# Ten tiles turned by VectorE in 32 by 32 blocks instead of by TensorE

## The chip, the core and the metric

The kernel runs on one core of one Trainium2 chip. The metric is the device time of one execution in microseconds (us). Engines are named as in the profile: PE is TensorE (PEld its weight loads), DVE is VectorE, ACT is ScalarE, POOL is GpSimd, SP is the engine that only issues transfers. PSUM is the memory that PE writes to, SBUF the working memory.

## What is computed

A graph attention layer on 2708 nodes of width 1024, all in fp32:

```
h   = relu(layernorm(x))
z   = (h Wq' + bq) (h Wk' + bk)' / 32            # only where adj is not 0
out = x + relu(softmax(z * adj, else -10000) (h Wv' + bv))
```

adj is 0 or 1 with about 4 ones in a row, so the kernel never forms the 2708 by 2708 matrix.

## The kernel before, in words

**Algebra.** Wq and Wk are first multiplied into one matrix M, so that q = h M is all that the scores need. For each node the rows h of its neighbours are gathered, their scores are dot products with q, and u is the weighted sum of those same rows. The result is u Wv. So two matrix products of 2688 by 1024 by 1024 remain on PE: "q units" (h M) and "o units" (u Wv).

**Tiles and units.** Nodes are sorted by degree and cut into 21 full tiles of 128 rows and a short one. Units 0 to 9 are q units, units 10 to 19 are o units, each with a pair of tiles. The o pairs follow the list `order` (L928): (6,5), (4,3), (2,0), (1,7) are units 10 to 13, (13,12), (11,10), (14,9), (15,16) units 14 to 17, (20,17) and (18,19) units 18 and 19. Tile 8 is `alone` and comes last.

**One unit.** A unit is a Strassen product of a 2 by 2 block of tiles: seven products of 8 PE instructions each. `multiply` (L982) runs them in this order, and calls `after(0)` to `after(6)` (L1172) around them: s2 (into bank Y), a12 (X), s4 (Z), s3 (Y), then a11 and s1 of the next unit (`opened`, L953), then a22 (Y). The left operands are made in the unit before by `blocks` (L677). Its `upper`, called at `after(0)`, turns tile xa: PE transposes eight 128 by 128 blocks into PSUM (`half_turned`, L397), and ACT copies them out as a11 and a12. Its `lower`, called at `after(2)`, does the same for xb; ACT copies a22 alone, and DVE makes s1 = a22 + a21 and s3 = a11 - a21 with a21 read from PSUM, then s2 = s1 - a11 and s4 = a12 - s2. In q units 1 and 2, s2 and s4 are made by POOL (`eng`, L701 and L702); in all later units by DVE.

**The results of a unit.** c11 and c21 leave their bank by ACT; c12 (L1063) is a DVE addition that reads bank Z, c22 (L1059) a DVE addition behind an ACT copy. There are four banks for X, Y, Z. The copy that starts bank Y of the next unit (`opened`, L961, on ACT) takes the bank that c12 sets free.

**The stream on DVE.** Scores (L826), weights (L840 to L873) and sums (L879) of all tiles form one sequence of steps, `attention` (L897), which `advance` (L937) deals out between the products: `share`, that is 19/7 us of estimated step time, at each `after` of an o unit. Each score is a pass over 1024 columns with two operands in SBUF (a gathered row block g and q), each sum another (g and u). The order of DVE's instructions is the order in which this code writes them (L1165); the other engines' order in units 4 to 19 is chosen by the scheduler. The first term of u is written by ACT (L871). POOL issues the gathers (L597) into 13 buffers; a gather waits for the step that read its buffer last.

**Keeping or reloading u.** When the last sum of tile t is done, `near` (L933) asks whether the tile's unit is at most two units ahead. If so, u stays in SBUF (`held`). If not, SP stores it to `u_dram` (L888) and `load_rows` (L1130) brings it back with one transfer of 128 rows of 4 KB (L1142). Ten tiles go that way: 6, 5, 4, 3, 2, 0, 1 and 20, 18, 19. `load_rows` for unit n+2 is called at `after(4)` of unit n, and before it a loop (L1214) advances the stream until both tiles are done, whatever `share` says. Rows live in seven buffers of 4 KB (`row_tile`, L198).

Of the kernel before, what the change touches and what calls it, by code (L numbers as in the profile page):

```python
# [15 lines left out]
ALU = mybir.AluOpType  # L16
AX = mybir.AxisListType

P = 128
# [13 lines left out]
NONE = 1e-30  # L33
FAR = 20.0
WIDE = 8
MOMENTS = (0, 1, 2, 3, 6, 7)
ROOT = 32
WARM = 11
# [25 lines left out]
def tile_preln_masked_attention(  # L64
# [12 lines left out]
    nc = tc.nc  # L77
    N, D = x.shape
# [25 lines left out]
    u_dram = dram.tile([FULL * P, D], FT, name="u_dram")  # L104
# [61 lines left out]
    t = 0  # L166
    while t < NT:
# [4 lines left out]
        t = e  # L172
# [25 lines left out]
    def row_tile(name):  # L198
        return work.tile([P, D], FT, tag="row", name=name, bufs=ROWS)
# [197 lines left out]
    def half_turned(xt, s):  # L397

        pt = psum.tile([P, 4, P], FT, tag="tp", name="pt")
        for c in range(4):  # L400
            k = s * 4 + c
            nc.tensor.transpose(pt[:, c, :], xt[:, k * P:(k + 1) * P], ident)  # L402
        return pt
# [187 lines left out]
    def small(name):  # L591
        return half.tile([P, NB], FT, tag="half", name=name, bufs=14)
# [8 lines left out]
    rows_of = {}  # L601
    FIRST = EARLY // 2
# [71 lines left out]

    behind = []

    def blocks(xa, xb, eng=None):  # L677


        ops = {}  # L680

        def held(name, bank):
            ops[name] = small(name).rearrange("p (c q) -> p c q", q=P)
            nc.scalar.copy(ops[name], bank)  # L684

        def put(name, a, b, op, eng=None):
            ops[name] = small(name).rearrange("p (c q) -> p c q", q=P)
            step = (eng or nc.vector).tensor_tensor(ops[name], a, b, op=op)  # L688
            if eng is None:
                behind.append(step)  # L690

        def upper():
            held("a11", half_turned(xa, 0))
            held("a12", half_turned(xa, 1))

        def lower():
            held("a22", half_turned(xb, 1))
            a21 = half_turned(xb, 0)
            put("s1", ops["a22"], a21, ALU.add)
            put("s3", ops["a11"], a21, ALU.subtract)  # L700
            put("s2", ops["s1"], ops["a11"], ALU.subtract, eng)  # L701
            put("s4", ops["a12"], ops["s2"], ALU.subtract, eng)  # L702

        return ops, upper, lower
# [170 lines left out]
    def sums(t):  # L875
        u, coef = us.pop(t)
        for s in range(0 if t in EMPTY else 1, K[t]):
            fill()
            chained(lambda: nc.vector.scalar_tensor_tensor(  # L879
                u, g_of[t][s], coef[:, at[t][s]:at[t][s] + 1], u, op0=ALU.mult, op1=ALU.add))  # L880
            free.append(g_of[t][s])
            yield 1.3
        fill()
        g_of.pop(t)
        if near(t):
            held[t] = u
        else:
            nc.sync.dma_start(u_dram[t * P:(t + 1) * P, :], u)  # L888
        done.add(t)
# [43 lines left out]
    def near(t):  # L933

        return t == alone or any(t in unit[1:] for unit in units[:now[0] + 3] if unit[0] == "o")
# [194 lines left out]
    def load_rows(unit):  # L1130
        kind, *pair = unit
        rows = []
        for t in pair:
            if t in held:
                rows.append(held.pop(t))
                continue
            rows.append(row_tile(f"{kind}r_{t}"))
            if kind == "q":
                gather(rows[-1], h_dram[:, :], t, SLOTS, P)
            else:  # L1140
                assert t in done, (t, done)
                nc.sync.dma_start(rows[-1], u_dram[t * P:(t + 1) * P, :])  # L1142
        return rows

    products = []
# [14 lines left out]
    for n, unit in enumerate(units):  # L1160
        kind, ta, tb = unit
        now[0] = n
        if n == FIRST:
            ordered.close()
            ordered.enter_context(tc.manual_schedule(engines={mybir.EngineType.DVE}))  # L1165
            nc.sync.dma_start(bp_dram, bp_sb[0:1, :])
        turn = n in (0, FIRST - 1)
        share = (20.0 if kind == "q" else 19.0) / 7
        nxt = units[n + 1] if n + 1 < len(units) else None
        results = (q_results if kind == "q" else o_results)(ta, tb)  # L1170

        def after(i):  # L1172
            if (n, i) in steps_ahead:
                follow(steps_ahead[n, i])
            if (n, i) == (2, 5):
                owe(8)
                owe(9)
                rows_of[FIRST] = load_rows(units[FIRST])
                owe(10)
                owe(6)  # L1180
                owe(7)
                rows_of[FIRST + 1] = load_rows(units[FIRST + 1])
                pooled.close()
            if (n, i) in ((FIRST, 1), (FIRST, 5)):
                ts_of_wv(i // 2, i // 2 + 2)
            if (n, i) == (FIRST, 5):
                next(stream)
            if (n, i) == (FIRST, 6):
                chain.append(behind[-1])
                next(stream)  # L1190
                nc.vector.tensor_tensor(bad, bad, total, op=ALU.not_equal)
            if (n, i) == (FIRST + 1, 6):
                marked(EARLY, NT)
            if (n, i) == (FIRST + 2, 4):
                nc.vector.tensor_scalar(msq, msq, MLIMIT, None, op0=ALU.is_gt)
            if n > FIRST + 1 or n == FIRST + 1 and i > 1:
                advance(share)
            if nxt is not None:

                if i == (3 if n == 0 else 4 if turn else 0):  # L1200
                    ops_of[n + 1] = blocks(*rows_of[n + 1], nc.gpsimd if n + 1 < FIRST - 1 else None)
                    with tc.issue_after(products[-1].ins) if n + 1 == FIRST else nullcontext():
                        ops_of[n + 1][1]()
                if i == (4 if n == 0 else 5 if turn else 2):
                    ops_of[n + 1][2]()
                    rows_of.pop(n + 1)
                    if n == last_q - 1:
                        all_rows()
                if i == 3:
                    banks_of[n + 1] = banks_for(bp_sb)  # L1210
                if i == 6 and n + 2 < FIRST:
                    natural_rows(n + 2)
                if i == (2 if n in (FIRST, last_q) else 4) and n + 2 > FIRST and n + 2 < len(units) and n + 2 not in rows_of:
                    while units[n + 2][0] == "o" and not done.issuperset(units[n + 2][1:]):  # L1214
                        advance(1.0)
                    rows_of[n + 2] = load_rows(units[n + 2])
            if (n, i) in steps_at:
                follow(steps_at[n, i])
            if (n, i) == (3, 4):
                searched()  # L1220
            if (n, i) == (3, 5):
                for s in range(8, HIGH):
                    for c in range(0, D, D // 4):
                        clear = nc.gpsimd.memset(slots[s][:, c:c + D // 4], 0.0)
                        tc.add_manual_dep(clear.ins, counted_at[-1].ins.name,
                                          mybir.DependencyInfo(mybir.DependencyClass.Sync, mybir.DependencyReason.DATA),
                                          reason="not beside the counts")
            if i == 3 and units[n - 1][0] == "o" and NT - 2 in units[n - 1][1:]:
                tail(NT - 1)
            if nxt is None and i == 1:  # L1230
                while alone not in done:
                    advance(1.0)
                r, = load_rows(("o", alone))
                single["turned"] = turned(r, "alone")
            if nxt is None and i == 3:
                single["banks"] = banks_for(bp_sb)
            if n == last_q - 1 and i == 4:

                nc.sync.dma_start(bp_sb, bv.to_broadcast([P, D]))
                nc.vector.tensor_sub(bp_sb[:, NB:], bp_sb[:, NB:], bp_sb[:, :NB])  # L1240

            for k, at in enumerate(((0, 0), (0, 1), (0, 3), (0, 4), (0, 5), (0, 6), (1, 2))):
                if (n - last_q, i) == at:
                    place, src = ((M[:, 0, 0], of_wv(0, 0)), (T[:, 0], tv_dram[0]), (T[:, 1], tv_dram[1]),
                                  (M[:, 1, 0], of_wv(1, 0)), (M[:, 1, 1], of_wv(1, 1)), (T[:, 2], tv_dram[2]),
                                  (T[:, 3], tv_dram[3]))[k]
                    nc.sync.dma_start(place, src)

        multiply(n, results, after)
# [231 lines left out]
```

## Time and profile before

| | |
|---|---|
| median of 3 runs | 644.58 us (644.18 to 644.96) |
| profiled execution, first to last instruction | span 641.9 us; no total is listed for this execution |
| busy: PE, DVE, POOL, ACT | 635.2, 521.9, 377.3, 279.6 us of the span |
| PE's granted clock | 9 of 10 or more in all 40 slices (mean 0.998) |
| DMA engines | 315 GB/s over the span |

An o or q unit lasts 25.78 us on PE: unit 9 begins at 346.70 us of the span, unit 19 at 604.55 us. In the rows of the profile, a line begins with its time and duration or with its source line and engine; `out<-in` are the program's tile names, xN is a count, and what stands in brackets or behind "<-" is how long the engine had been idle and what released it. `pt<-ident,or` are the transposes of reloaded tiles, `pt<-ident,u` those of held ones.

### The profile page before, as it was taken

How to read it: one execution, taken by the hardware profiler on the slowest of the kernel's cores; microseconds unless marked ns; L12 is line 12 of the kernel's file. 1: busy time of each engine (PE TensorE's matmuls, PEld its weight loads, DVE VectorE, ACT ScalarE, POOL GpSimd, SP SyncE). 2: the span in 40 equal slices, each digit the busy share in tenths (PEclk: the TensorE clock that was granted, in tenths of full speed). 3: DMA queues.
4: the chain of work that ended last, by engine and by line, in shares of the span. 5: the costliest groups of instructions: out<-in, count | busy, mean ns of one | idle time of the engine just before them, and what ended most of it. 6: DMA issues, size and time to landing. Idle time of an engine off the chain costs nothing.

```text
span 641.9 us, 6381 instructions
## 1 busy us (share of the span) xinstructions
PE 635.2 (99%) x1731; PEld 326.2 (51%) x1731; DVE 521.9 (81%) x1014; ACT 279.6 (44%) x426; POOL 377.3 (59%) x400
## 2 busy tenths in 40 slices
PE   9999999999999999999999999999999999999996
PEld 5777766444544444444444454454454444444442
DVE  5999788997895755998888959997999989989121
ACT  3539974849775622423223132433342344333300
POOL 2649960875858457755735525665685856872431
PEclk9999999999999999999999999999999999999999
DMA  8999997598798969998977998988898989995542
GB/s 338 407 366 314 345 346 295 189 358 301 264 358 317 363 201 404 355 359 257 322 260 275 419 416 267 327 272 255 240 328 272 283 331 304 281 285 125 146 139 95
DMA packets 61986, 189.02 MB, mean 294 GB/s; under 512 B 10701, under 2 KB 11037, under 8 KB 61048
## 3 DMA queue, kind: packets, MB, share of 16 engines
q0 software_dynamic: 27888, 84.95, 41.6%
q1 hardware_dynamic: 29994, 89.36, 37.7%
q10 hardware_dynamic: 4062, 14.24, 5.9%
q8 instruction: 16, 0.26, 0.2%
q14 instruction: 26, 0.21, 0.1%
HBM read 159.81 MB, written 42.31 MB: 315 GB/s over the span
## 4 chain that ended last, share of the span: by engine, by line
PE 98%; DMA 1%; DVE 0%; POOL 0%; POOLq 0%; issue 0%
PE ps L948 45%; PE psy L948 32%; PE ps_y L463 6%; PE pt L402 6%; PE ps_x L463 4%; PE ps_z L463 4%; DMA wlow<-in_wq_dram 1%; PE ps_h L1153 0%; PE ps_v L581 0%; DVE y_alone L1297 0%; POOL out_dram L1281 0%; POOLq L1303 0%; PE ps_all L664 0%; PE ps_in L662 0%; PE ps_b L728 0%
## 5 line engine op out<-in xcount | busy, mean ns | idle before, releaser
L597 POOL DMA_INDIRECT g<-h_dram,tab x105 | 124.8, 1188 | 70.4 <-ACT u L871 19.1
L948 PE MATMUL ps<-M,a 128*128 128x512 f32 x320 | 144.0, 593 | 0.0
L948 PE MATMUL psy<-wlow,s 128*128 128x512 f32 x320 | 143.9, 592 | 0.0
L826 DVE SCALAR_TENSOR_TENSOR junk<-g,pq 128x1024 uint8<-128x1024 f32 x93 | 114.0, 1226 | 9.8 <-DMA g<-h_dram,tab 7.3
L879 DVE SCALAR_TENSOR_TENSOR u<-g,coef,u 128x1024 f32<-128x1024 f32 x79 | 101.4, 1283 | 5.6 <-ACT u L871 3.7
L948 PEld LDWEIGHTS ps<-M,a 128*128 128x128 f32 x320 | 59.3, 190 | 68.0 <-issue 67.4
L948 PEld LDWEIGHTS psy<-wlow,s 128*128 128x128 f32 x320 | 59.2, 190 | 66.8 <-issue 65.8
L376 DVE FIND_INDEX8 at<-ones,adj 128x8 uint32<-128x685 f32 (+1 forms) x88 | 74.5, 865 | 0.0
L948 PE MATMUL psy<-wlow,a 128*128 128x512 f32 x160 | 71.9, 592 | 0.0
L948 PE MATMUL ps<-M,s 128*128 128x512 f32 x160 | 71.9, 592 | 0.0
L948 PE MATMUL ps<-wlow,s 128*128 128x512 f32 x160 | 71.9, 592 | 0.0
L355 ACT ACTIVATE sized<-adj 128x2708 uint8<-128x2708 f32 (+1 forms) x22 | 54.3, 2468 | 7.7 <-DMA adj<-in_adj_dram 6.4
L285 POOL TENSOR_TENSOR hsum<-hsum,x 128x256 f32<-128x256 f32 (+1 forms) x56 | 38.6, 726 | 26.3 <-DVE wlow L431 22.3
L1047 POOL DMA_INDIRECT y<-in_x_dram,tab x19 | 33.5, 1763 | 30.8 <-ACT taken L1013 11.2
L948 PEld LDWEIGHTS psy<-wlow,a 128*128 128x128 f32 x160 | 30.4, 190 | 38.3 <-issue 37.8
L948 PEld LDWEIGHTS ps<-wlow,s 128*128 128x128 f32 x160 | 30.4, 190 | 38.3 <-issue 37.6
L948 PEld LDWEIGHTS ps<-M,s 128*128 128x128 f32 x160 | 30.3, 190 | 38.1 <-issue 37.4
L778 POOL DMA_INDIRECT out_dram<-y,tab x21 | 28.4, 1353 | 19.3 <-DMA y<-in_x_dram,tab 11.6
L684 ACT COPY a<-pt 128x512 f32<-128x512 f32 x60 | 33.4, 590 | 3.1 <-PE pt L402 3.1
L597 POOL DMA_INDIRECT M<-h_dram,tab x20 | 24.2, 1212 | 13.4 <-ACT u L871 4.7
L688 DVE TENSOR_TENSOR s<-a,pt 128x512 f32<-128x512 f32 x40 | 25.6, 681 | 7.8 <-ACT a L684 7.8
L871 ACT ACTIVATE u<-g,coef 128x1024 f32<-128x1024 f32 x16 | 18.4, 1149 | 27.1 <-DVE coef L870 26.3
(238 smaller groups left out, 847.9 us busy)
## 6 DMA issues: line engine op xcount, KB each, us to landing
adj<-in_adj_dram SPq DMA_DIRECT2D x21, 1354.0 KB, 12.0
x<-in_x_dram SPq DMA_DIRECT2D x21, 512.0 KB, 8.0
h_dram<-x ACTq DMA_DIRECT2D x21, 512.0 KB, 7.2
q_late<-q SPq DMA_DIRECT2D x12, 512.0 KB, 6.9
pq<-q_late SPq DMA_DIRECT2D x12, 512.0 KB, 4.8
u_dram<-u SPq DMA_DIRECT2D x10, 512.0 KB, 6.5
or<-u_dram SPq DMA_DIRECT2D x10, 512.0 KB, 8.2
g<-in_wv_dram SPq DMA_DIRECT2D x16, 256.0 KB, 8.3
```

The lines of the kernel that those rows point to most:

```text
L285: small.append(nc.gpsimd.tensor_add(hsum[:n, cols], hsum[:n, cols], xt[:n, cols]))
L355: nc.scalar.activation(sized[:n], a[:n, :, :PW], AF.Abs, accum_out=total[:n, t:t + 1])
L376: nc.vector.max_index(at[:n, k - first_k, g, :], ones[:n, 0:8], a[:n, g, :])
L402: nc.tensor.transpose(pt[:, c, :], xt[:, k * P:(k + 1) * P], ident)
L463: mm = nc.tensor.matmul(bank, a_tile(o + H * a[0], a[1], i), b(o), start=first and o == 0, stop=(o == H - 1), skip_group_check=True)
L597: return nc.gpsimd.indirect_dma_start(out=dst, out_offset=None, in_=src, in_offset=off, bounds_check=N - 1, oob_is_err=False)
L684: nc.scalar.copy(ops[name], bank)
L778: to = nc.gpsimd.indirect_dma_start(out=out, out_offset=bass.IndirectOffsetOnAxis(ap=ptab.bitcast(U32)[:n, t, SLOTS:SLOTS + 1], axis=0), i ...
L826: chained(lambda: nc.vector.scalar_tensor_tensor(junk, g_of[t][s], 1.0, tq[t], op0=ALU.mult, op1=ALU.mult, accum_out=zall[:, t, s:s + 1]))
L879: chained(lambda: nc.vector.scalar_tensor_tensor(u, g_of[t][s], coef[:, at[t][s]:at[t][s] + 1], u, op0=ALU.mult, op1=ALU.add))
L948: mm = nc.tensor.matmul(bank, a[:, c, :], b[:, c, :], start=False, stop=(c == 3), skip_group_check=True)
L1047: return nc.gpsimd.indirect_dma_start(out=y[:n], out_offset=None, in_=x, in_offset=off, compute_op=ALU.add)
```

## The change

The ten tiles of the list FACED, which are those ten, are turned without PE.

- When u of such a tile is done, ACT copies it (128 by 1024) to a new row tile v with its columns in quarter order: column c*128 + a*32 + r goes to a*256 + c*32 + r. ACT also issues the store of v to `u_dram`; SP no longer does.
- `load_rows` brings it back with four transfers on SP in place of one. Transfer a fills partitions 32a to 32a+31 with quarter a of the columns, in pieces of 1 KB.
- In `blocks`, one DVE transpose of 128 by 512 in 32 by 32 blocks writes each of a11 and a12 (tile xa), or a22 and a21 (tile xb). a21 is written into the buffer of s3, and s3 is then made in place.
- If one tile of the unit is faced, POOL makes s2 and s4 instead of DVE.
- `share` is lowered by 0.75/7 us for each faced tile of the next unit.

```diff
+QUADS = 4
+QP = P // QUADS
+FACED = (6, 5, 4, 3, 2, 0, 1, 20, 18, 19)
...
+    def by_quarters(dst, rows):
+        faced.append(dst)
+        for a in range(QUADS):
+            cols = slice(a * D // QUADS, (a + 1) * D // QUADS)
+            nc.sync.dma_start(dst[a * QP:(a + 1) * QP, :].rearrange("r (g j) -> r g j", g=QUADS),
+                              rows[:, cols].rearrange("(g r) j -> r g j", r=QP))
+    def faces(dst, xt, lo, hi):
+        return nc.vector.transpose(dst.rearrange("p c (g r) -> p g c r", r=QP),
+                                   xt.rearrange("p (g c r) -> p g c r", g=QUADS, r=QP)[:, :, lo:hi])
...
+        def faced_half(name, xt, s):
+            ops[name] = small(name).rearrange("p (c q) -> p c q", q=P)
+            faces(ops[name], xt, s * 4, s * 4 + 4)
         def upper():
-            held("a11", half_turned(xa, 0))
-            held("a12", half_turned(xa, 1))
+            for s, name in enumerate(("a11", "a12")):
+                if is_faced(xa):
+                    faced_half(name, xa, s)
+                else:
+                    held(name, half_turned(xa, s))
         def lower():
+            if is_faced(xb):
+                faced_half("a22", xb, 1)
+                faced_half("s3", xb, 0)
+                put("s1", ops["a22"], ops["s3"], ALU.add)
+                behind.append(nc.vector.tensor_sub(ops["s3"], ops["a11"], ops["s3"]))
+            else:
...
-        if near(t):
+        if t in FACED:
+            v = row_tile(f"v_{t}")
+            nc.scalar.copy(v.rearrange("p (a c r) -> p c a r", a=QUADS, r=QP),
+                           u.rearrange("p (c a r) -> p c a r", a=QUADS, r=QP))
+            nc.scalar.dma_start(u_dram[t * P:(t + 1) * P, :], v)
+        elif near(t):
...
-                nc.sync.dma_start(rows[-1], u_dram[t * P:(t + 1) * P, :])
+                if t in FACED:
+                    by_quarters(rows[-1], u_dram[t * P:(t + 1) * P, :])
+                else:
+                    nc.sync.dma_start(rows[-1], u_dram[t * P:(t + 1) * P, :])
...
+        if nxt is not None and nxt[0] == "o":
+            share -= 0.75 / 7 * len(set(nxt[1:]) & set(FACED))
...
-                    ops_of[n + 1] = blocks(*rows_of[n + 1], nc.gpsimd if n + 1 < FIRST - 1 else None)
+                    ops_of[n + 1] = blocks(*rows_of[n + 1], nc.gpsimd if n + 1 < FIRST - 1 or any(
+                        is_faced(xt) for xt in rows_of[n + 1]) else None)
```

More of the change, by code (lines that the diff above doesn't have):

```diff
@@ L675, in tile_preln_masked_attention, with is_faced @@
     behind = []
+    faced = []
+    def by_quarters(dst, rows):
[7 more added lines that the diff above has]
+                                   xt.rearrange("p (g c r) -> p g c r", g=QUADS, r=QP)[:, :, lo:hi])
+    def is_faced(xt):
+        return any(xt is y for y in faced)
     def blocks(xa, xb, eng=None):
@@ L690, in put @@
                 behind.append(step)
+        def faced_half(name, xt, s):
+            ops[name] = small(name).rearrange("p (c q) -> p c q", q=P)
+            faces(ops[name], xt, s * 4, s * 4 + 4)
         def upper():
-            held("a11", half_turned(xa, 0))
-            held("a12", half_turned(xa, 1))
-        def lower():
[L697 to L700, printed above, removed]
+            for s, name in enumerate(("a11", "a12")):
[3 more added lines that the diff above has]
+                    held(name, half_turned(xa, s))
+        def lower():
+            if is_faced(xb):
[4 more added lines that the diff above has]
+            else:
+                held("a22", half_turned(xb, 1))
+                a21 = half_turned(xb, 0)
+                put("s1", ops["a22"], a21, ALU.add)
+                put("s3", ops["a11"], a21, ALU.subtract)
             put("s2", ops["s1"], ops["a11"], ALU.subtract, eng)
```

## The prediction

> **What bounds the kernel now.** First the page's chain of work that ended last, then the list of what PE waited for.
>
> ```profile
> PE 98%; DMA 1%; DVE 0%; POOL 0%; POOLq 0%; issue 0%
> PE ps L948 45%; PE psy L948 32%; PE ps_y L463 6%; PE pt L402 6%; PE ps_x L463 4%; PE ps_z L463 4%; DMA wlow<-in_wq_dram 1%; PE ps_h L1153 0%; PE ps_v L581 0%; DVE y_alone L1297 0%; POOL out_dram L1281 0%; POOLq L1303 0%; PE ps_all L664 0%; PE ps_in L662 0%; PE ps_b L728 0%
> PE ps_y L498 <- POOL hsum L112: 1.2, 1, 1.2
> PE ps_x L463 <- DMA wlow<-in_wq_dram: 0.3, 1, 0.3
> ```
>
> PE is the whole chain, and after its start it waits for nobody: 1.2 and 0.3 us are all. An instruction taken off PE shortens the kernel as long as the others keep up. What the transposes of reloaded tiles cost is read from PE's order of time in unit 9:
>
> ```profile
> L402 PE MATMUL pt<-ident,or x80: 272/273/273, 346.7 to 583.8; 128*128 128x128 f32 x80
> ...
> 346.70 1.04 PE L402 MATMUL pt<-ident,or 128*128 128x128 f32 x8
> 347.57 3.60 PE L948 MATMUL psy<-wlow,s 128*128 128x512 f32 x8
> ```
>
> The 273 ns overlap; from the eight's start to the next product's is 0.87 us. So one reloaded tile holds PE for 0.87 us.
>
> The second view is DVE near the end of unit 15, because DVE has the most work behind PE. c12 of that unit (L1063) must come before ACT starts the next bank Y (L961), and PE needs that bank for unit 16's first product.
>
> ```profile
> 524.77 0.68 DVE L1063 TENSOR_TENSOR u<-ps,u 128x512 f32<-128x512 f32 x1
> ...
> 526.47 0.57 ACT L961 COPY psy<-ps 128x512 f32<-128x512 f32 x1
> ...
> 528.07 3.60 PE L948 MATMUL psy<-wlow,s 128*128 128x512 f32 x8
> ```
>
> The copy ends at 526.47 + 0.57 = 527.04 and PE uses it at 528.07. **DVE is 1.0 us from holding up PE here**, though no list of waits says so. The reason is the loop that finishes the tiles of unit n+2: in units 13 and 14 it deals out steps beyond `share` (9 and 8 turns, counted along the code of the stream). That order also means that a smaller `share` earlier takes nothing from DVE before this point; the loop puts the steps back.
>
> **What the change removes.** PE: 80 transposes, 10 x 0.87 = 8.7 us. If all else keeps up, 644.58 - 8.7 = 635.9. (The profiled span is 641.9; 2.7 us of the median lie around it or in the spread, and nothing in the change touches them. So I take differences off the median.) Seven of the ten tiles (units 9 to 12 turn 6, 5, 4, 3, 2, 0, 1) come before the narrow place: PE reaches it 7 x 0.87 = 6.1 us earlier.
>
> **What DVE gains and loses up to there.** No DVE transpose stands in the trace. The nearest rows, and those of the moved additions:
>
> ```profile
> L224 DVE BATCH_NORM_STATS2 st<-x 128x6 f32<-128x512 f32 x30 | 18.7, 665 | 0.0
> L688 DVE TENSOR_TENSOR s<-s,a 128x512 f32<-128x512 f32 x18 | 12.3, 684 | 0.0
> ...
> 352.44 1.28 DVE L688 TENSOR_TENSOR s<-a,pt 128x512 f32<-128x512 f32 x2
> ...
> 10.89 0.75 DVE L517 TENSOR_SCALAR acc_b<-wlow,bq_sb 128x1024 f32<-128x1024 f32 x1
> ...
> 590.13 1.28 DVE L879 SCALAR_TENSOR_TENSOR u<-g,coef,u 128x1024 f32<-128x1024 f32 x1
> ```
>
> A 128x512 pass takes 1.28/2 = 0.64 us when two follow each other, with one operand about the same (0.665 alone). I take 0.64 for a transpose. The bounds are half of the fastest 1024-column pass, 0.37, and one pass of twice the columns, 1.28. Two transposes for each of seven tiles: 14 x 0.64 = 9.0 us (5.2 to 17.9). s1 and s3 stay at their price. s2 and s4 of four units leave DVE: 8 x 0.684 = 5.5 us less.
>
> [...]
>
> **Moving s2 and s4 to POOL is not free for DVE.** This is how two such POOL additions met DVE in unit 1, and what the same DVE form takes alone:
>
> ```profile
> 67.74 0.29 DVE L389 TENSOR_TENSOR cand<-first,at 128x128 f32<-128x128 f32 x1
> ...
> 132.93 1.26 DVE L389 TENSOR_TENSOR cand<-first,at 128x128 f32<-128x128 f32 x1
> 134.22 1.31 DVE L390 SCALAR_TENSOR_TENSOR cand<-at,cand 128x128 f32<-128x128 uint32 x1
> ...
> 132.78 1.26 POOL L688 TENSOR_TENSOR s<-s,a 128x512 f32<-128x512 f32 x1
> 134.12 1.27 POOL L688 TENSOR_TENSOR s<-a,s 128x512 f32<-128x512 f32 x1
> ```
>
> DVE's two-operand passes stretched from 0.29 to 1.26 and (taking L390 alone as equal) 1.31: DVE lost 2.0 us to two POOL additions. Scores and sums have two SBUF operands too and fill DVE, so I charge 2.0 for each of four units, 8.0 us. Bounds: 0, if POOL's additions meet transposes, PSUM reads or idle time, and 8 x 1.27 = 10.2. The move thus costs DVE more than it saves.
>
> [...]
>
> **What of it DVE's idle time swallows.** DVE's waits from unit 9 to this place:
>
> ```profile
> DVE junk L826 <- DMA g<-h_dram,tab: 7.3, 5, 2.1
> DVE s L688 <- ACT a L684: 3.4, 2, 2.2
> DVE u L1063 <- PE ps L948: 1.7, 1, 1.7
> DVE u L879 <- ACT u L871: 1.2, 1, 1.2
> DVE m L861 <- ACT w L860: 0.9, 2, 0.5
> DVE junk L826 <- DMA M<-h_dram,tab: 0.9, 1, 0.9
> DVE q L1029 <- PE psy L948: 0.2, 1, 0.2
> ```
>
> The 3.4 us for ACT's copies go, since DVE now makes those operands. The 1.9 for PE vanish when DVE is late. Of the 8.2 for gathers I take three quarters, 6.1: some gathers wait for a sum that is itself later. Together 11.4; the bounds are 5.3 (no gather) and 13.5 (all).
>
> **Sum.** DVE comes later against PE by 6.1 + 9.0 - 5.5 + 8.0 - 11.4 = 6.2 us. 1.0 is free, so PE waits 5.2 us between units 15 and 16. Of 8.7 remain 3.5: **641.1 us**.
>
> **After unit 15** the last three tiles take 2.6 us off PE, and DVE gets 6 x 0.64 - 4 x 0.684 + 4.0 = 5.1 us. What could be late next is tile 8: its last sum and its transposes are
>
> ```profile
> 604.55 1.04 PE L402 MATMUL pt<-ident,u 128*128 128x128 f32 x8
> ```
>
> The sum quoted above at 590.13 ends at 591.4: 13.1 us of slack against 2.6 + 5.1 + 1.0. No second stall.
>
> **What lies beside other work.** ACT loses 16 copies and gains 10 passes:
>
> ```profile
> L684 ACT COPY a<-pt 128x512 f32<-128x512 f32 x60 | 33.4, 590 | 3.1 <-PE pt L402 3.1
> L871 ACT ACTIVATE u<-g,coef 128x1024 f32<-128x1024 f32 x16 | 18.4, 1149 | 27.1 <-DVE coef L870 26.3
> ...
> u_dram<-u SPq DMA_DIRECT2D x10, 512.0 KB, 6.5
> or<-u_dram SPq DMA_DIRECT2D x10, 512.0 KB, 8.2
> ...
> tab<-tab_dram SPq DMA_DIRECT2D x1, 72.0 KB, 2.4
> ```
>
> 10 x 1.15 - 16 x 0.59 = +2.1 us on an engine that is busy 44%, covered. But ACT waits for the last sum before each copy, and the bank copies and results queue behind it; it already waits 26.3 us that way for L870 without harm, so I charge nothing, with up to 1.2 us (one pass) at unit 15, where tile 20's copy falls near L961. The store's issue leaves SP, which gets 40 loads to issue instead of 10, on a queue that does nothing else but issue. v takes one of seven row buffers, but sets u's free a store (6.5 us) earlier. Smaller pieces: 72 KB went in rows of 72 bytes, about a thousand pieces, in 2.4 us, so 512 pieces of 1 KB add at most about that to 8.2. Tile 20 is the tightest: its last sum starts at 526.51; plus 1.3, 1.2, 6.5 and 10.6 it is back at 546, and unit 17 turns it at 552.98.
>
> ```profile
> 526.51 1.28 DVE L879 SCALAR_TENSOR_TENSOR u<-g,coef,u 128x1024 f32<-128x1024 f32 x1
> 552.98 1.04 PE L402 MATMUL pt<-ident,or 128*128 128x128 f32 x8
> ```
>
> **The rivals.**
>
> *DVE keeps up: 635.9 to 637.5.* If POOL's additions cost a third of 8.0 and all waits for gathers are swallowed, 6.2 - 5.3 - 2.1 is below the 1.0 that is free. For it: the additions wait for s1, and s3 or a transpose may run beside them. Against: the waits listed above, 15.6 of some 180 us, are nearly all that DVE leaves idle. 0.16.
>
> *The whole gain is eaten: about 644.6.* Halfway to the bad bounds, with 9.1 for POOL and 8.4 for idle time, DVE is 10.3 us late and the stall is 9.3: 645.2. For it: both terms are chosen, not seen. Against: it needs both at once. 643.3 to 645.9 has 0.13.
>
> *POOL comes late with s2 and s4: about 650, slower.* POOL works in order, and a gather in front waits for its buffer. Before, it did so in unit 10:
>
> ```profile
> 382.80 0.99 POOL L597 DMA_INDIRECT g<-h_dram,tab  x1 [8.79 <-ACT u L871]
> 390.12 1.03 POOL L597 DMA_INDIRECT g<-h_dram,tab  x1 [6.33 <-DMA or<-u_dram]
> ...
> 383.52 1.28 DVE L688 TENSOR_TENSOR s<-a,pt 128x512 f32<-128x512 f32 x2 [2.17 <-ACT a L684]
> ...
> 398.27 1.04 PE L402 MATMUL pt<-ident,or 128*128 128x128 f32 x8
> ```
>
> s1 is ready near 384.2 there (half of 1.28 after 383.52), and PE needs s2 at 398.27: 14 us, less 4 x 0.87 by which PE is early, so it decides from 10.6 us of queue. A wait of 8.8 with five gathers of 1.03 behind it is 14, a stall of 3.4 a unit; in four units 13.7, and 635.9 + 13.7 = 649.6. Against: the scheduler puts gathers where it expects buffers to be free. 0.13.
>
> *The transposes take 1.28: about 650, slower.* 14 x 0.64 = 9.0 more. 0.08.
>
> **How the numbers follow.** The forecast has 0.50, its own range 638 to 643.2. Faster by over 0.2% (1.3 us, about what this kernel's measurement can tell from none) is 0.50 + 0.16 = 0.66, same 0.13, slower 0.21. The range 636.5 to 647.5 leaves out half of the first rival and most of the last two.
>
> **What would show it.** PE without `or` transposes and a wait between units 15 and 16 (or 14 and 15) for ACT's Y copy or DVE; DVE transposes near 0.64; scores and sums of 2 us or more beside POOL's additions; no wait for reloaded rows. Wrong would be: no PE wait at all, a PE wait for POOL, or transposes over 0.9.

## The result, and the profile after

| | before | after |
|---|---|---|
| median, us | 644.16 (643.73 to 645.33, 22 runs) | 643.62 (641.80 to 647.66, 22 runs) |
| profiled span, us | 641.9 | 640.7 |
| busy PE, DVE, POOL, ACT, us | 635.2, 521.9, 377.3, 279.6 | 630.0, 535.9, 398.4, 282.2 |

The ratio is 0.9997, interval 0.9986 to 1.0008: no difference. The 641.1 us that were forecast lie inside the range, but the clear gain is missing, and the single runs spread over 6 us where those of the kernel before spread over 1.6. The profiled execution took 642.46 us, 1.2 less than the median; the longer ones have no profile.

The chain of work that ended last and the list of PE's waits, both of the changed kernel, stand against the first fence of the prediction:

```profile
PE 18%; DVE 16%; issue 12%; DMA 9%; POOL 4%; ACT 0%; POOLq 0%; DVEq 0%
```

```profile
PE ps L987 <- DMA M<-in_wv_dram: 2.8, 1, 2.8
...
PE ps L987 <- DVE s L709: 1.2, 1, 1.2
PE pt L405 <- DVE u L913: 0.3, 1, 0.3
```

PE no longer is the chain. The longest wait is one that the prediction didn't have: for a load of weights. PE's order of time shows where, first in the changed kernel, then in the kernel before (start, duration, source line, bracketed idle time and what ended it):

```profile
371.50 3.60 PE L987 MATMUL psy<-wlow,s 128*128 128x512 f32 x8
377.86 5.40 PE L987 MATMUL ps<-M,a 128*128 128x512 f32 x8 [2.77 <-DMA M<-in_wv_dram]
383.10 3.60 PE L987 MATMUL ps<-M,s 128*128 128x512 f32 x8
```

```profile
377.67 3.60 PE L948 MATMUL ps<-M,a 128*128 128x512 f32 x8
381.10 3.60 PE L948 MATMUL ps<-M,s 128*128 128x512 f32 x8
```

A product takes 3.43 us from start to start (377.67 to 381.10). Here, in unit 10, the first of the o units, 371.50 to 377.86 is 6.36 and 377.86 to 383.10 is 5.24: **4.74 us are lost in unit 10**, 2.93 by the wait and 1.81 because the product behind it runs slowly. DVE's lateness shows only in two small places, 505.52 (0.44 lost) and 521.48 (1.32): together 6.5 us.

To compare profiles without what happens before 324 us, take the distance between two rows of PE's order of time: the sum of x rows (L1153 before, L1195 after), which ends the first part, and the last group of products. Kernel before, then after:

```profile
324.38 1.88 PE L1153 MATMUL ps_h<-hsum,ones 128*128 128x512 f32 x4
...
629.68 7.03 PE L948 MATMUL ps<-M,T_alone 128*128 128x512 f32 x16
```

```profile
325.15 1.88 PE L1195 MATMUL ps_h<-hsum,ones 128*128 128x512 f32 x4
...
628.39 7.03 PE L987 MATMUL ps<-M,T_alone 128*128 128x512 f32 x16
```

305.30 against 303.24: 2.06 gained, and 8.7 less 6.5 is 2.2. The account of this profile closes. The same distance is used for the experiments below, as "PE's stretch".

Why the weights are late: SP's queue in order of time, after and before.

```profile
348.64 3.83 SPq L687 DMA_DIRECT2D or<-u_dram  x7
355.92 0.34 SPq L1292 DMA_DIRECT2D wlow<-tv_dram  x1
362.20 0.34 SPq L1061 DMA_DIRECT2D q_late<-q  x1
362.63 2.60 SPq L1292 DMA_DIRECT2D M<-in_wv_dram  x2
```

```profile
351.20 0.32 SPq L1247 DMA_DIRECT2D wlow<-tv_dram  x1
355.51 3.77 SPq L1247 DMA_DIRECT2D M<-in_wv_dram  x2
359.71 0.33 SPq L1022 DMA_DIRECT2D q_late<-q  x1
```

Seven quarter loads now stand in front of the block of T, which is issued at 355.92 instead of 351.20; both blocks of M follow the store of unit 9's q tile instead of preceding it and are issued from 362.63 instead of 355.51, 7.1 us later. And SP waits for landings, which it never did in this window (335 to 400 us) before. In the first of these rows quarter loads wait for blocks of T to land, in the second weights wait for quarter loads, in the third weights wait for the store of a q tile:

```profile
SPq L687 <- DMA wlow<-tv_dram: 8.0, 2, 4.6
...
SPq L1292 <- DMA or<-u_dram: 3.5, 2, 1.8
SPq L1292 <- DMA q_late<-q: 3.4, 1, 3.4
```

The second difference is in the DMA engines. The table by stretches (length of the stretch; busy us of PE, PEld, DVE, ACT and POOL, each with its count; granted clock, DMA share, GB/s), before and after:

```profile
360.00:370.00 10.00, 10.00 (x25) 4.46 (x24) 9.60 (x12) 1.16 (x2) 3.95 (x4) 1.00 1.02 419
```

```profile
360.00:370.00 10.00, 10.00 (x25) 4.47 (x24) 9.89 (x9) 1.46 (x2) 8.27 (x7) 1.00 1.05 310
370.00:380.00 10.00, 7.23 (x16) 2.91 (x15) 9.83 (x18) 2.71 (x6) 0.99 (x1) 0.96 1.02 421
380.00:390.00 10.00, 10.00 (x22) 4.28 (x21) 8.31 (x13) 2.96 (x4) 4.94 (x4) 0.87 1.02 419
```

Here the DMA engines are full (a share of 1) in both kernels; this is the stretch in which the weights of the o units are loaded. While quarter loads run, they move 310 GB/s instead of 419 at the same fullness. The queue that SP feeds and the loads themselves, after (queue: packets, MB, share of 16 engines; issues: count, size, us to landing):

```profile
q1 hardware_dynamic: 32874, 84.12, 37.5%
...
or<-u_dram SPq DMA_DIRECT2D x40, 128.0 KB, 12.2
...
wlow<-tv_dram SPq DMA_DIRECT2D x4, 1024.0 KB, 18.4
```

By the median a quarter load lands 12.2 us after its issue where a whole tile took 8.2, and a block of T takes 18.4 instead of 11.9.

### The profile page after: what moved, and what is told of

Its sections match the earlier page's. It is cut to its first block, busy times and chain, and to the rows that moved or that the text cites. A ratio compares the mean times of both kernels' runs of the same rounds, so it can differ in the third digit from the quotient of the medians.

```text
span 640.7 us, 6299 instructions
## 1 busy us (share of the span) xinstructions
PE 630.0 (98%) x1651; PEld 318.6 (50%) x1651; DVE 535.9 (84%) x1022; ACT 282.2 (44%) x420; POOL 398.4 (62%) x412
## 3 DMA queue, kind: packets, MB, share of 16 engines
q1 hardware_dynamic: 32874, 84.12, 37.5%
## 4 chain that ended last, share of the span: by engine, by line
PE 18%; DVE 16%; issue 12%; DMA 9%; POOL 4%; ACT 0%; POOLq 0%; DVEq 0%
PE ps L987 10%; PE psy L987 7%; DVE junk L860 6%; DVE u L913 6%; DMA g<-h_dram,tab 3%; DMA pq<-q_late 3%; POOL g L600 2%; DMA or<-u_dram 2%; DMA qr<-h_dram,tab 2%; DVE s L709 1%; POOL M L600 1%; DMA pq<-q_dram,tab 1%; PE pt L405 1%; POOL qr L602 0%; DVE a L692 0%
## 5 line engine op out<-in xcount | busy, mean ns | idle before, releaser
L600 POOL DMA_INDIRECT g<-h_dram,tab x105 | 128.0, 1219 | 53.4 <-issue 19.2
L987 PE MATMUL ps<-M,a 128*128 128x512 f32 x320 | 145.8, 599 | 2.8 <-DMA M<-in_wv_dram 2.8
L860 DVE SCALAR_TENSOR_TENSOR junk<-g,pq 128x1024 uint8<-128x1024 f32 x93 | 115.9, 1246 | 3.5 <-DMA g<-h_dram,tab 1.0
L913 DVE SCALAR_TENSOR_TENSOR u<-g,coef,u 128x1024 f32<-128x1024 f32 x79 | 106.1, 1343 | 5.2 <-ACT u L905 3.1
L987 PEld LDWEIGHTS psy<-wlow,a 128*128 128x128 f32 x160 | 30.3, 190 | 38.5 <-issue 36.8
L987 PEld LDWEIGHTS ps<-M,s 128*128 128x128 f32 x160 | 30.3, 190 | 38.3 <-issue 37.5
L1086 POOL DMA_INDIRECT y<-in_x_dram,tab x19 | 31.0, 1633 | 14.7 <-issue 4.4
L600 POOL DMA_INDIRECT M<-h_dram,tab x20 | 22.9, 1145 | 12.8 <-ACT u L905 4.7
L616 POOL DMA_INDIRECT tab_dram<-tab,pos_i x22 | 22.4, 1018 | 11.7 <-DVE pos_i L676 6.2
L266 ACT ACTIVATE x<-x,r 128x1024 f32<-128x1024 f32 (+1 forms) x22 | 25.8, 1232 | 6.1 <-POOL r L256 6.1
L905 ACT ACTIVATE u<-g,coef 128x1024 f32<-128x1024 f32 x16 | 18.4, 1148 | 21.9 <-DVE coef L904 20.8
## 6 DMA issues: line engine op xcount, KB each, us to landing
adj<-in_adj_dram SPq DMA_DIRECT2D x21, 1354.0 KB, 12.2
or<-u_dram SPq DMA_DIRECT2D x40, 128.0 KB, 12.2
```

The lines of the kernel that those rows point to most:

```text
L266: nc.scalar.activation(xs[i][:n], xs[i][:n], AF.Relu, bias=r[:n, 4, i:i + 1], scale=r[:n, 3, i:i + 1])
L600: return nc.gpsimd.indirect_dma_start(out=dst, out_offset=None, in_=src, in_offset=off, bounds_check=N - 1, oob_is_err=False)
L616: put = nc.gpsimd.indirect_dma_start(out=tab_dram[lo >= EARLY][:, :], out_offset=bass.IndirectOffsetOnAxis(ap=pos_i[:n, t:t + 1], axis=0), ...
L860: chained(lambda: nc.vector.scalar_tensor_tensor(junk, g_of[t][s], 1.0, tq[t], op0=ALU.mult, op1=ALU.mult, accum_out=zall[:, t, s:s + 1]))
L905: nc.scalar.activation(u, g_of[t][0], AF.Copy, scale=coef[:, at[t][0]:at[t][0] + 1])
L913: chained(lambda: nc.vector.scalar_tensor_tensor(u, g_of[t][s], coef[:, at[t][s]:at[t][s] + 1], u, op0=ALU.mult, op1=ALU.add))
```

## The experiments

Three theories: **A**, SP's queue (four issues for each tile, and their places) holds the weights back; **B**, the prediction's own, VectorE is late; **C**, the quarter loads in pieces of 1 KB take DMA engine time. The sets ran on different chips: on that of sets 3 and 4 the kernel before takes 644 us, on those of sets 1, 2 and 5 it takes 648. Ratios are to the kernel before in the same set. They must not be compared across the two kinds: the changed kernel itself reads 0.9962 on one kind and 0.9999 on the other.

### Set 1 (kernel before 648.67 us)

**m10_early.** The load of M's second block (half 1, block 0) from unit 9's place 4 to place 3; nothing else changes its order.

```
-((0, 0), (0, 1), (0, 3), (0, 4), (0, 5), (0, 6), (1, 2))
+((0, 0), (0, 1), (0, 3), (0, 3), (0, 5), (0, 6), (1, 2))
```

> The changed kernel with one entry of SP's queue moved: the second Wv block of the first o unit (M, half 1, block 0) is loaded ahead of the store of unit 9's q tile, as in the kernel before, instead of behind it. Everything else has the same order. Theory A (SP's queue holds the weights back): the stall of 4.7 us in unit 10 shrinks to under 1 us, the median falls from 643.6 to 639.5 to 641.0 and the runs spread less. Theory B (the one predicted: VectorE's lateness takes the gain): the time won in unit 10 comes back as waits for VectorE's s1 or sums around unit 16, 643.0 to 644.2. Theory C (the loads land late whenever they are issued, because the quarter loads fill the DMA engines): the product still waits, 643 to 645.

Measured 0.9964 (0.9942 to 0.9986). The wait didn't go; it moved to the next block, which still stood behind the store: PE waits 3.2 us for M and loses 6.4 there and at the product behind it. So the place of this one load isn't the whole of it.

**one_load.** In `load_rows`:

```
-by_quarters(rows[-1], u_dram[t * P:(t + 1) * P, :])
+faced.append(rows[-1])
+nc.sync.dma_start(rows[-1], u_dram[t * P:(t + 1) * P, :])
```

> The changed kernel with one load of 128 rows of 4 KB for each of the ten u tiles in place of four quarter loads; VectorE's transposes and all the rest are as they were, so the o rows are computed from tiles whose blocks stand in the wrong places. Theory A: T block 1 of Wv is issued near 350 instead of 356 and the stall in unit 10 goes, 639.0 to 641.0. Theory B: 643.0 to 644.2, with waits for VectorE between units 14 and 16. Theory C: landing of the u loads falls from 12.2 to about 8.2 us, and the time with it, 639 to 641; then m10_early has to stay slow.

0.9962 (0.9944 to 0.9980). No wait for weights, but up to 2.9 us at once for VectorE's sums. Without a control in this set it could be read neither way; it was run again in set 4.

**s24_dve.** `blocks(..., nc.gpsimd if n + 1 < FIRST - 1 else None)`, as before the change.

> The changed kernel with s2 and s4 of the o units left on VectorE, as in the kernel before. Theory B, with the recorded prices (VectorE loses 2.0 us to GpSimd's pair in each unit and saves 0.79 to 1.10 us of its own additions): VectorE is better off by some 2.5 to 4 us, and the time falls to 641.5 to 642.5. Theory A: the stall in unit 10 stays, 643 to 644.5.

0.9939 (0.9916 to 0.9962), with the wait for M (3.2 us) still there.

**traffic.** `is_faced` returns False, and `share` is as before.

> The changed kernel with only its copies, stores and quarter loads: the ten tiles are turned by TensorE as in the kernel before, from the tiles as the quarter loads leave them (so the o rows are computed from tiles whose blocks stand in the wrong places), and s2 and s4 are VectorE's. No TensorE time is saved. Theory A: the kernel before plus the loss in unit 10, 647.5 to 650. Theory B: 644 to 645, no difference to the kernel before. Theory C: as A, and the weights land late also where they are issued on time.

1.0140 (1.0107 to 1.0174): 659 us. PE's waits from 320 to 600 us in this kernel:

```profile
PE pt L405 <- DMA or<-u_dram: 5.2, 1, 5.2
PE ps L987 <- DMA M<-in_wv_dram: 1.3, 2, 1.1
PE ps L987 <- DVE s L709: 1.0, 1, 1.0
```

**Copies, stores and quarter loads alone make the kernel 1.4% slower**, although VectorE has neither transposes nor GpSimd's additions beside it. B, which gave 644 to 645 for it (1.000 here), has no account of that. A and C have the direction, but the 647.5 to 650 that they gave (about 1.005 to 1.008) fall short of it too. The medians differ by 10.3 us; PE's waits in this list make 7.5, and behind the longest the granted clock is 0.52, 0.50, 0.50 and 0.77 in the four stretches of 2 us from 410 to 418: eight transposes and a product take 1.73 and 5.51 us there from start to start (411.02, 412.75, 418.26) instead of 0.87 and 3.43, 2.9 more.

### Set 2 (kernel before 647.95 us)

**after_again**, the changed kernel:

> The changed kernel once more, unaltered, beside the others of this set on one chip: 0.998 to 1.002 of the kernel before, as at first. What the others are compared with.

0.9962 (0.9942 to 0.9982), not the 0.9997 of the first measurement. On this chip PE comes to unit 10 later (the sum of x rows starts at 327.73 instead of 325.15), and waits 0.6 us for M and 0.3 for T there instead of 2.8. The profiled execution is the fastest of its twelve (642.52, median 645.43), and m10_early and s24_dve, on another chip of this kind, waited 3.2 us for M, so the short wait need not be the rule here. As far as two chips of one kind compare, set 1's m10_early and one_load had thus won nothing over the changed kernel.

**four_natural.** In `by_quarters`:

```
-cols = slice(a * D // QUADS, (a + 1) * D // QUADS)
-nc.sync.dma_start(dst[a * QP:(a + 1) * QP, :].rearrange("r (g j) -> r g j", g=QUADS),
-                  rows[:, cols].rearrange("(g r) j -> r g j", r=QP))
+nc.sync.dma_start(dst[a * QP:(a + 1) * QP, :], rows[a * QP:(a + 1) * QP, :])
```

> The changed kernel with each u tile still loaded by four transfers of 32 partitions, at the same places of SP's queue, but each of them 32 whole rows of 4 KB instead of 128 pieces of 1 KB; the o rows are computed from tiles whose blocks stand in the wrong places. Theory A (number of issues and their place on SP's queue): nothing moves, 0.998 to 1.002 of the kernel before and the product of unit 10 still waits for M. Theory C (pieces of 1 KB cost DMA engine time): the wait for M goes or shrinks under 1 us, the share of the hardware queue falls from 37.5% to about 35.6%, 0.994 to 0.997.

0.9970 (0.9956 to 0.9984), no better than its control. Its profile: M's blocks are issued at 368.59, later than in any kernel above, and PE doesn't wait for them; it waits 4.0 us for VectorE's sums and 1.6 for s1. The place in the queue alone thus didn't make a wait here, which speaks against A. The absent wait and the time fit what was recorded for C, but they are nearly the same in the control and so say little. C's own sign, the pieces, failed: the queue's share was to fall to about 35.6%, and it is 36.4%, near the control's 36.8%. And the full DMA engines still move less than 419 GB/s:

```profile
360.00:370.00 10.00, 10.00 (x25) 4.46 (x24) 9.79 (x10) 0.59 (x2) 8.94 (x6) 1.00 1.03 324
```

The control moves 342 GB/s in this stretch, and one_load_2 of set 4, with one load for each tile, 417. So the lower rate is there with whole rows of 4 KB too: it goes with the split into four transfers of 32 partitions, and no run shows that the pieces of 1 KB add much to it.

**one_load_s24** (one load, and s2 and s4 on VectorE):

> The changed kernel with one load of 128 whole rows for each u tile and with s2 and s4 of the o units left on VectorE; the o rows are computed from tiles whose blocks stand in the wrong places. If DMA time in units 9 to 12 and GpSimd's hold on VectorE are two separate losses, both gone, most of TensorE's 8.7 us arrives: 0.987 to 0.991. If the one only hid the other's place (theory B alone), it is no better than s24_dve, 0.994 or above.

0.9930 (0.9908 to 0.9953), short of the expected 0.987 to 0.991. PE waits 2.1 us for VectorE's sums.

**six_s24.** `FACED = (2, 0, 1, 20, 18, 19)`, and s2 and s4 on VectorE.

> The changed kernel with only six tiles turned by VectorE (2, 0, 1, 20, 18, 19: none is reloaded while the Wv weights are loaded for units 9 and 10), s2 and s4 on VectorE. TensorE saves 6 x 0.87 = 5.2 us. Theory C, and A: no wait for M in unit 10, 0.991 to 0.994. Theory B with the transposes' 0.64 us: about the same, since VectorE has fewer of them before unit 15; so a result above 0.996 would speak for a cause not yet named.

0.9974 (0.9954 to 0.9995), a miss, and above 0.996, which by its expectation speaks for a cause not yet named. The profile shows no wait for weights, but 1.2 us for s1, 1.1 for a sum and 0.4 for an ACT copy; PE's stretch is 303.39, so 1.91 of the 5.2 are gained.

### Set 3 (kernel before 644.03 us)

**before_again**, unaltered:

> The kernel before, unaltered, for a profile on the chip of the other runs: ratio 1. On the first chip TensorE had no stall of its own between 300 and 600 us. If the changed kernel reads 0.996 here and 0.9997 there because the kernel before loses something here, its profile shows stalls of TensorE after 300 us of some 2 to 3 us; if not, it shows none.

0.9999 (0.9991 to 1.0008), no stall after 300 us. It came to a chip of the first kind, so what the kernel before does where it takes 648 us has no profile.

**one_load_short.** On one_load:

```
-faces(ops[name], xt, s * 4, s * 4 + 4)
+faces(ops[name][:, 0:1], xt, s * 4, s * 4 + 1)
+nc.scalar.copy(ops[name][:, 1:4], xt[:, s * NB + P:(s + 1) * NB].rearrange("p (c q) -> p c q", q=P))
```

> The kernel with one load of whole rows for each u tile, with VectorE turning only the first 128 of the 512 columns of each half; ScalarE copies the other 384 unturned. The blocks of the o rows are wrong as in the kernel it is built on, and three quarters of them unturned. VectorE gets back most of 0.65 us at each of 20 transposes, 14 of them before unit 15. Theory B (VectorE's time is what is short once the weights come in time): the waits for VectorE's sums and s1 around 500 us, 5 to 6 us in all, shrink under 1.5 us and the time falls from 0.996 to 0.988 to 0.991. If VectorE's time isn't short there (its waits come from the order of its queue alone, or from late DMAs): 0.995 or above.

0.9920 (0.9907 to 0.9932), just above what was expected. PE's stretch is 300.04, 5.26 gained; waits of 1.9 and 1.2 us for VectorE stay, more than the 1.5 that were expected. Beside one_load_2 of set 4 (0.9936, the same chip) the shorter transposes are worth about 1 us (1.6 in PE's stretch). Between 340 and 500 us they take VectorE 2.9 us instead of 7.3, but its waits grow by as much: for gathers from 2.9 to 5.6, by 1.2 for the ACT copies that this run adds, by 0.5 for PE.

**s24_m10** (m10_early and s24_dve together):

> The changed kernel with s2 and s4 of the o units on VectorE and the load of M's second block ahead of the store of unit 9's q tile. If GpSimd's hold is worth what the two pairs with and without it said (0.9962 to 0.9939, 0.9962 to 0.993), 0.993 to 0.994; the place of the load alone has shown nothing, so no more than that. If both differences were scatter, 0.996.

0.9986 (0.9970 to 1.0001), a miss: 3.1 us of waiting for M's two blocks in unit 10. The two pairs of which the expectation spoke stood on other chips.

**three_s24.** `FACED = (20, 18, 19)`, s2 and s4 on VectorE.

> The changed kernel with only tiles 20, 18 and 19 turned by VectorE, s2 and s4 on VectorE: nothing is added to VectorE before unit 17, and no quarter load runs beside the Wv weights. TensorE saves 3 x 0.87 = 2.6 us. Theory B: nothing is eaten, 0.996 (0.9955 to 0.9965). Theory C: the same, since the DMA engines' crowded stretch is untouched. If the transposes cost even here, after the stream's end, 0.998 or above.

0.9960 (0.9947 to 0.9973), 641.68 us, runs within 0.8 us. As expected. PE's stretch is 302.68: 2.62 gained, 3 x 0.87 is 2.61.

### Set 4 (kernel before 643.96 us, the chip of set 3)

**after_third**, the control:

> The changed kernel, unaltered, as the control of this set: 0.9997 where the kernel before takes 644 us, 0.996 where it takes 648 us.

0.9999 (0.9981 to 1.0018). Waits of 3.2 for M and 0.8 for T in unit 10.

**one_load_2**, the edit of one_load:

> One load of whole rows for each of the ten u tiles once more (blocks of the o rows in the wrong places), beside its control. If the two losses stand one behind the other for the same time (VectorE's lateness takes over what the late weights leave free): within 0.002 of after_third, with the waits for VectorE's sums and s1 around 500 us grown to 4 to 6 us. If they add: 0.004 to 0.007 below after_third, and the waits around 500 us as in the profile of the changed kernel, 1.8 us.

**0.9936 (0.9923 to 0.9950), 640.00 us**, its five runs between 639.81 and 640.40. Its order of time on PE:

```profile
324.75 1.88 PE L1196 MATMUL ps_h<-hsum,ones 128*128 128x512 f32 x4
...
497.04 3.60 PE L987 MATMUL psy<-wlow,s 128*128 128x512 f32 x8
503.52 1.94 PE L405 MATMUL pt<-ident,u 128*128 128x128 f32 x8 [2.89 <-DVE u L913]
505.25 4.24 PE L987 MATMUL ps<-M,a 128*128 128x512 f32 x8
509.33 3.17 PE L987 MATMUL ps<-M,s 128*128 128x512 f32 x7
...
626.42 7.03 PE L987 MATMUL ps<-M,T_alone 128*128 128x512 f32 x16
```

The weights are in time, and VectorE is late where the control had been made to wait already: 3.05 from 497.04 to 503.52 (6.48 less 3.43), 0.85 at the transposes (1.73 less 0.87), 0.65 at the product behind them, and 0.45 at 489.22: 5.0 lost. PE's stretch is 301.67, 3.63 gained; 8.7 less 5.0 is 3.7. The queue's share is 35.9%. Both of the sentences recorded for this run were half right: the waits near 500 us grew as for losses one behind the other, and the time fell by 0.0063 as for losses that add. The medians lie 3.4 us apart and the two profiled executions 2.9, of which 2.0 are in PE's stretch (the control's is 303.69). The control's runs scatter from 641.5 to 648.5 and those with one load don't; what the slower ones lose has no profile.

**after_short** (one_load_short's edit, with quarter loads):

> The changed kernel with its quarter loads, in which VectorE turns only 128 of the 512 columns of each half and ScalarE copies the other 384 unturned (so those parts of the o rows are computed from unturned blocks): VectorE gets time back, the loads stay. If the losses stand one behind the other: the wait for M in unit 10 stays at 2 to 4 us and the waits around 500 us go, 0.001 to 0.003 below after_third. If VectorE's time is all that counts: 0.992, as with one load.

1.0003 (0.9987 to 1.0020). Less work for VectorE wins nothing while the quarter loads are there. Its waits:

```profile
PE ps L988 <- DMA M<-in_wv_dram: 3.2, 1, 3.2
PE pt L405 <- DVE u L914: 1.7, 1, 1.7
...
PE ps L988 <- DVE s L709: 1.2, 1, 1.2
```

The wait for M stays; those for VectorE stay too, since VectorE now waits itself (3.6 us for quarter loads, 6.9 for PE's products between 330 and 500 us).

**four_s24.** `FACED = (1, 20, 18, 19)`, s2 and s4 on VectorE.

> Only tiles 1, 20, 18 and 19 turned by VectorE, s2 and s4 on VectorE. TensorE saves 4 x 0.87 = 3.5 us; the one tile before unit 15 costs VectorE 1.3 us, less than the 6.5 to 7 us that it waits for gathers in the kernel before. All of it kept: 0.9945. If one tile before unit 15 already stalls TensorE: 0.996, as three_s24.

**0.9951 (0.9937 to 0.9964), 640.92 us, the fastest of the versions that leave every block of u in its place**: faster than the kernel before and than the changed one. Two rows of its order of time:

```profile
325.31 1.88 PE L1195 MATMUL ps_h<-hsum,ones 128*128 128x512 f32 x4
...
627.11 7.03 PE L987 MATMUL ps<-M,T_alone 128*128 128x512 f32 x16
```

301.80: 3.50 gained, 4 x 0.87 is 3.48. PE has no wait after 300 us.

### Set 5 (kernel before 648.35 us)

**four_natural_2:**

> Four transfers of 32 whole rows of 4 KB for each u tile, at the places of the quarter loads on SP's queue (blocks of the o rows in the wrong places). If the pieces of 1 KB are the cause: 0.993 to 0.995, as with one load (0.9936), and no wait for M in unit 10. If the number of issues and their place are the cause: 0.998 to 1.001 as the changed kernel, M's blocks again issued behind 362 us and waited for by 2 to 3 us. If both, between. This holds where the kernel before takes 644 us; where it takes 648 us, both kernels read 0.996 to 0.997 and it settles nothing.

0.9983 (0.9965 to 1.0001), on a chip of the other kind, where it settles nothing, as was said beforehand. Again no wait for M, and 4.5 us for VectorE's sums.

**five_s24.** `FACED = (0, 1, 20, 18, 19)`, s2 and s4 on VectorE.

> Tiles 0, 1, 20, 18 and 19 turned by VectorE, s2 and s4 on VectorE. TensorE saves 5 x 0.87 = 4.4 us. If VectorE and the loads still keep up: 0.9935 to 0.994. If the second tile before unit 15 starts to stall TensorE: 0.995 or above, and waits for VectorE around 500 us.

0.9968 (0.9949 to 0.9987), above what was expected. PE's stretch is 302.05, 3.25 of the 4.4 gained; the one wait after 300 us is 0.5 for an ACT copy, none is for weights or VectorE's sums. On this kind of chip its ratio can't be set against that of four_s24.

## Why the prediction was wrong

Step by step:

- **PE's 8.7 us were right.** One tile is worth 0.87: three gave 2.62 and four 3.50 where nothing else stalled.
- **Transposes at 0.64 us were right.** VectorE's rows in the changed kernel, by tile (ns: least, median, most) and in order of time:

```profile
L692 DVE STREAM_TRANSPOSE a<-or x16: 669/704/712, 347.9 to 590.7; 128x512 f32<-128x512 f32 x16
```

```profile
347.93 1.30 DVE L692 STREAM_TRANSPOSE a<-or 128x512 f32<-128x512 f32 x2
```

  0.65 when two follow each other.
- **GpSimd's price of 8.0 us for VectorE was about right.** One pair of additions in the changed kernel and the two sums beside it:

```profile
357.04 4.49 DVE L913 SCALAR_TENSOR_TENSOR u<-g,coef,u 128x1024 f32<-128x1024 f32 x2
```

```profile
356.58 1.67 POOL L709 TENSOR_TENSOR s<-s,a 128x512 f32<-128x512 f32 x1
358.33 2.12 POOL L709 TENSOR_TENSOR s<-a,s 128x512 f32<-128x512 f32 x1
```

  Two sums take 2.6 alone (2 x 1.28): 1.9 lost, and GpSimd's own additions stretch from 1.27 to 1.67 and 2.12. For the whole way, VectorE's groups between 340 and 500 us in one_load_2 and in the kernel before:

```profile
L913 DVE SCALAR_TENSOR_TENSOR u<-g,coef,u 128x1024 f32<-128x1024 f32 x41 | 55.5, 1354 | 2.1 <-ACT u L905 1.2
L860 DVE SCALAR_TENSOR_TENSOR junk<-g,pq 128x1024 uint8<-128x1024 f32 x42 | 53.4, 1271 | 3.6 <-DMA g<-h_dram,tab 2.9
...
L902 DVE SCALAR_TENSOR_TENSOR w<-w,keys 128x7 f32<-128x7 f32 (+4 forms) x8 | 3.4, 423 | 0.3 <-ACT w L876 0.3
```

```profile
L879 DVE SCALAR_TENSOR_TENSOR u<-g,coef,u 128x1024 f32<-128x1024 f32 x41 | 52.6, 1283 | 2.2 <-ACT u L871 1.2
L826 DVE SCALAR_TENSOR_TENSOR junk<-g,pq 128x1024 uint8<-128x1024 f32 x41 | 50.1, 1223 | 7.9 <-DMA g<-h_dram,tab 7.3
...
L868 DVE SCALAR_TENSOR_TENSOR w<-w,keys 128x7 f32<-128x7 f32 (+4 forms) x8 | 1.3, 162 | 0.3 <-ACT w L842 0.3
```

  41 x 71 ns, 42 x 48 ns and 8 x 261 ns are 2.9 + 2.0 + 2.1 = 7.0 us. In s24_m10, on the same chip with these additions on VectorE, the sums and scores of these groups are back at 1283 and 1220 ns, so the stretch is GpSimd's. Against the 5.5 us that leave VectorE the move costs it 1.5 net. Whether the move loses against keeping s2 and s4 on VectorE was expected to show in the times and didn't: s24_m10 and s24_dve stand in other sets than the runs that they would be compared with, or the intervals touch.
- **Idle time that swallows 11.4 us: about right.** The waits for gathers into g fell from 7.3 to 2.9 in the rows just shown; those into M (0.9), for ACT's copies (3.4) and for PE (1.9) are gone in one_load_2. That makes 10.6.
- **VectorE late, and 5.2 us of stall: it happens where the loads are out of the way, but that the size fits is partly luck.** one_load_2 loses 5.0 and gains 3.63 where 3.5 were forecast. The place is a little earlier than named, inside unit 15: not c12 by way of ACT's copy of Y releases PE, but the last sum of a held tile that PE turns there for unit 16. And the sum treats the idle time that VectorE swallows as fixed. With 4.4 us less of transposes (one_load_short) it would leave about 0.8 of the 5.2; 3.4 were left (8.7 less 5.26), because VectorE's waits, for gathers above all, grew by those 4.4.
- **The step that failed is the one that charged the loads nothing**: SP would get "40 loads to issue instead of 10, on a queue that does nothing else but issue", and smaller pieces would add at most about 2.4 us to a landing of 8.2. That queue also carries the weights of the first o units and stores that wait for VectorE: the store at 362.20 waited 5.9 us for it, and M's blocks went out behind it, from 362.63. From 350 to 390 us the DMA engines that the queue feeds are full (a share of 1.02 to 1.05). With quarter loads a transfer of a u tile lands 4.0 us later and a block of T 6.5 later, M's blocks are issued 7.1 us later, and PE lost 4.7 us in unit 10. A wait of PE for weights stands in neither of the prediction's lists of signs. The same kernel with one load in place of four is 0.6% faster than the changed one beside it. The DMA share of that stretch, 1.02 in the kernel before, is nowhere in the prediction.

What is shown: the quarter loads, as against one load of the same bytes, take the gain on the chip where the kernel before takes 644 us. What stays open is how that divides between the DMA engines (310 GB/s while quarter loads run, 324 with four transfers of whole rows, 417 with one) and the place and the waits in SP's queue (M's blocks behind a store, weights waiting for landings). In four_natural M's blocks, issued latest of all, were there at most 10.6 us later (PE takes them at 379.21 without a wait), where in the changed kernel 15.2 us passed (377.86), so the place in the queue alone doesn't make the wait; but this run and its repetition came to chips of the kind on which the one profile of the changed kernel hardly waits for weights. Why the changed kernel wins 0.4% there and nothing here is open as well. In after_again's profile PE's stretch is 300.60, 4.7 us less than in the kernel before here, though that is its fastest run; on those chips the first part of the profiled kernels ends at 327.7 to 330.1 us instead of 324.4 to 325.4, and the kernel before has no profile there.

## What to carry to other kernels

Before charging a transfer at nothing, look at the DMA share of the very stretch in which it runs and at everything behind it on its queue: here, at a share of 1.02 to 1.05, with each load of a u tile split in four, a block of T landed 18.4 us after its issue instead of 11.9, M's blocks were issued 7.1 us later, and PE lost 4.7 us in unit 10. A shift of work between engines is best taken in the units where all of it is hidden: four tiles outside the crowded stretch brought 0.5% where ten brought nothing. And a late step can cover another: a fix for the second wait shows nothing until the first is gone.

## What the runs showed of the hardware that was not expected

- **Loads split by partitions.** Ten tiles (5.2 MB) in quarters take 37.5% x 640.7 = 240.3 us of the SP queue's time on 16 engines, with one load each 35.9% x 638.6 = 229.3 (one_load_2): 11 us more. At the 419 GB/s of the full stretch the bytes alone would take 12.5 us. On one chip of the other kind the figures are 36.8% x 640.8 = 235.8 in quarters (after_again), 36.4% x 645.4 = 234.9 in four transfers of whole rows (four_natural) and 35.6% x 642.9 = 228.9 with one load (one_load_s24). There nearly all of the extra time comes with the four transfers of 32 partitions, and hardly any with the pieces of 1 KB.
- **A short wait cost PE twice.** After the wait of 2.77 us the granted clock is 0.79, 0.50 and 0.86 in the three stretches of 2 us from 378 to 384: 1.70 us of full clock are missing, and the product that waited takes 5.24 us instead of 3.43. The length of the wait alone doesn't decide: 1.7 us are missing after waits of 2.13 (one_load_s24) and 2.89 (one_load_2), 3.4 after 3.2 (m10_early) and 3.20 (s24_dve), and none after 2.89 (four_natural) and 3.19 (after_short), where the clock stays at 1.00.
- **Waits for landings on the issuing queue.** With 40 loads of u tiles to issue, SP's issue of a load waited, by the releasers that the profile infers, for the landing of an earlier transfer to or from another tile (3.5 us for quarter loads, 3.4 for a q store); with 10 such loads (the kernel before, one_load_2) it never did in that window.
